# Turning gathered rows on VectorE through DRAM, and moving contexts, key shifts and column sums in a fused cross-attention and mixture-of-experts kernel

## The chip, the cores and the metric

The kernel runs on one core of a Trainium2 chip. The metric is the time of one execution on the device in microseconds (us); the median of several runs counts. The core has five engines that each work through a queue of their own, in order: TensorE (PE), VectorE (DVE), ScalarE (ACT), GpSimd (POOL) and SyncE (SP, which here only issues DMAs). They wait for one another through semaphores. In the profile "PEld" is the loading of weights into TensorE, which overlaps its products.

## The reference

```python
# attention, residual
x = x + x_m          # query = ctx @ Wq.T + bq ; key = ctx @ Wk.T + bk
                     # attention = softmax(query @ key.T) ; x_m = layernorm(x) @ attention.T
# feed-forward on h = layernorm(x): 8 experts, 2 of them for each token
scores = sigmoid(h @ gate_w.T)
_, sel = top_k(scores + expert_bias, 2)
routed_in = h[tok_idx] * scores_sorted[:, None]
routed_out = grouped_swiglu(routed_in, w1, w2, w3, num_tokens_per_expert)   # bf16
shared = silu(h @ sw1.T) * (h @ sw3.T) @ sw2.T                              # f32
x = x + shared.at[tok_idx].add(routed_out)
```

x is 4 batches of 1024 rows of 1024 (f32), the context 4 x 1024 x 512, the head 128 wide, the hidden width 704.

## The kernel before

The kernel has three stages, one after the other on TensorE.

The attention stage (0 to about 650 us) works on tiles of 128 rows, numbered g = 0 to 31, eight to a batch b. It loops over 16 pairs of tiles (p, with g = 2p, and i the place of g in its batch). `product` multiplies a pair by the batch's turned attention matrix `aT` in seven products of halves (`seven`, a scheme that saves the eighth product by adding and subtracting halves): the first and second use the halves themselves and the sums `one`, the third `two`, the fifth the difference that overwrites `b12`, the seventh `four`. After product k the function `then(k)` adds the result to x (line 453), and `between(k)` runs everything else: a step for the tile pair before (its statistics spread over partitions: `masked` on VectorE, `spread` on TensorE, line 485; its turning, `normed` on ScalarE and `turn` on VectorE, line 503; its gate), routing of the pair before that (`route`, some twenty small VectorE instructions, and `weights_of`), loads for the next pair, and the next batch's attention: `looked` (energies on TensorE, line 346, and their maximum on VectorE), `softened` (the exponential on ScalarE), `scaled`, `turned`.

In the last pair of a batch (`last`) the queries and keys of the batch after the next are made: `queries` returns a generator, `half_queries`, whose steps are the products of one half of the context (`pq`, line 329), then its shift by the bias into `qT` and `kT` on VectorE (lines 334 and 336). The contexts come by `load_context` (tiles `ct`, 256 KB each, two buffers for each half of the width). The energies of the next pair need `kT` and the PSUM banks of `pq`.

The column sums of a batch come from `first_sums` (t0), `second_sum` (t1), and `last_sums` (b12 in place, then `four`), on VectorE. PE, DVE, ACT, POOL and SP follow the order of the program here; nothing reorders it.

The shared stage (to about 1459 us) computes the shared expert in f32, in eight slots s of 512 rows: `up(s)` with five rounds f of seven products of 256 columns, and two `down_pair`s. At the same time the rows for the routed experts are collected, by the generator `turns`, one step at each of k = 0, 2 and 4 of a round and at k = 3 of a down pair, from s = 2 on. A step gathers 128 listed rows (bf16, 1024 wide, with the token's number behind) from `xrows` into `xgt` through POOL, turns an earlier block by a DMA transpose from SP (line 1145) into a half `xh` of 256 rows, stores a filled half to `xturned` in DRAM (line 1137), and takes the tokens' numbers out on VectorE (line 1140). There are 92 blocks: 23 slots of four. In a round, VectorE adds `one += pb` (line 1082) after the fourth product and `five += pa` (line 1085) after the fifth; the seventh product writes to `pa` again. `hidden_sums` is eight VectorE additions after the fourth round and again after `up`.

POOL also rewrites the experts' weights in DRAM as bf16 (`pieces`, `convert`, line 255): five experts during the attention stage, three in the first two slots of the shared stage.

The routed stage (to the end) works through the 23 slots of one expert each: it loads the turned rows `xTb`, gathers the expert's weights (line 890), computes in bf16, and adds to the output by indirect DMAs.

Of the kernel before, what the change touches and what calls it, by code (L numbers as in the profile page):

```python
# [83 lines left out]
def xattn_moe_kernel(ctx: ExitStack, tc: tile.TileContext, x, ctxT, wqT, wkT, bqk, gwT, ebias,  # L84
# [30 lines left out]
    tokens_of = [cp.tile([P, NQ], I32, name=f"toks_{i}") for i in range(NS)]  # L115
    xturned = [dram.tile([P, KC, SLOT], BF16, name=f"xturned_{i}") for i in range(NS)]
# [117 lines left out]
    with ExitStack() as a:  # L234
# [14 lines left out]
        def pieces(experts):  # L249

            for e in experts:
                rows = slice(e * P, (e + 1) * P)
                for c in range(KC):
                    cols = slice(c * W13, (c + 1) * W13)
                    nc.gpsimd.dma_start(w13b[rows, cols], w13[rows, cols], max_dma_last_dim=8192)
                    yield
# [122 lines left out]
        def first_sums(b):  # L379
            b11, b12, b21, b22 = quarters(b)  # L380
            one, two = (p4.tile([P, HALF, 512], F32, tag=f"t{i}", name=f"t{i}_{b}")
                        for i in range(2))
            nc.vector.tensor_tensor(one, b12, b11, ALU.subtract)
            t_sums[b] = one, two

        def second_sum(b):
            one, two = t_sums[b][:2]
            nc.vector.tensor_tensor(two, quarters(b)[3], one, ALU.subtract)

        def last_sums(b):  # L390

            b11, b12, b21, b22 = quarters(b)
            four = p3.tile([P, HALF, 512], F32, tag="t4", name=f"t4_{b}", bufs=1)
            two = t_sums[b][1]
            t_sums[b] += four,
            yield
            nc.vector.tensor_tensor(b12, b22, b12, ALU.subtract)
            yield
            nc.vector.tensor_tensor(four, b21, two, ALU.subtract)
# [238 lines left out]
        load(0)  # L638
        with tc.manual_schedule(engines=vector_scalar | {mybir.EngineType.SP}):
# [26 lines left out]
            load(1)  # L666
            norms[1] = statistics(xin[1], "1_1")
            for m in range(LT + 2):
# [8 lines left out]
                if m == LT + 1:  # L677
                    halves = queries(1)
                    next(halves)
                    next(halves)  # L680
                    to_turn(1)
# [6 lines left out]
            for _ in halves:  # L688
                pass
# [3 lines left out]
            first_sums(0)  # L693
            second_sum(0)
# [4 lines left out]
            for p in range(NT // 2):  # L699
# [26 lines left out]
                looked(i)  # L726
                softened(i)
                if i == 0:
                    later = last_sums(b)
                    next(later)  # L730

                def between(k):
                    if 0 < k < NQ + 2:
                        next(converting, None)
                    if k == 0:
                        first_norm(g + 1)
                        if p:
                            masked(g - 2)
                        if i == 0 and b > 0:
                            second_sum(b)  # L740
                        if p > 1:
                            routing[g - 4] = route(g - 4, lgs.pop(g - 4))
                            rows[g - 4] = weights_of(g - 4, routing[g - 4][1])
                        if g + 2 < NT:
# [3 lines left out]
                        if last:  # L748
                            ask_contexts(b + 2, (0, 1))
                    elif k == 1:  # L750
                        if p:
                            spread(g - 2)
                        if ahead:
                            scaled(b + 1, i, on_scalar=True)
                        if p > 1:
                            for v in range(G):
                                weighted(g - 4 + v, *rows[g - 4][v])
                    elif k == 2:
# [9 lines left out]
                        if g + 2 < NT:  # L768
                            load(g + 3)
# [5 lines left out]
                        if i == 0:  # L775
                            next(later)
# [14 lines left out]
                    elif k == 4:  # L791
# [8 lines left out]
                        if i == 0:  # L800
                            next(later, None)
                        if g >= NT - LT:
                            weights_block(2 * (p % 4) + 1)
                    elif k == 5:
# [4 lines left out]
                        if g + 2 < NT:  # L809
                            first_norm(g + 2)  # L810
                            tokens(g + 3)
                            units[0] = row_sums(g + 2)
                    elif k == 6:
# [4 lines left out]
                        if ahead and i + 2 == LT:  # L818
                            first_sums(b + 1)
                        if last:  # L820
                            for _ in halves.pop():
                                pass
                        back(g)
                        back(g + 1)
                        if g + 2 < NT:
                            norms[g + 3] = statistics(xin[g + 3], f"1_{g + 3}")
# [223 lines left out]
    with shared, tc.manual_schedule(engines=vector_scalar | {mybir.EngineType.SP}):  # L1050
# [68 lines left out]
        def turns():  # L1119

            blocks = list(itertools.product(range(NS), range(NQ)))
            asked = []

            def ask(s, q):
                xg = tr.tile([P, ROW], BF16, tag="xg", name=f"xgt_{s}_{q}", bufs=4)
                gather(xg.bitcast(I32), xrows, li[:, s, q : q + 1])
                asked.append(xg)

            for b in blocks[:2]:
                ask(*b)  # L1130
            yield
            done = None
            for j, (s, q) in enumerate(blocks):
                if j + 2 < len(blocks):
                    ask(*blocks[j + 2])
                if done:
                    nc.sync.dma_start(*done)
                    done = None
                xg = asked.pop(0)
                nc.vector.tensor_tensor(tokens_of[s][:, q : q + 1], xg[:, D : D + 2].bitcast(I32),  # L1140
                                        beyond[:, s, q : q + 1], ALU.bitwise_or)
                h, v = divmod(q, 2)
                if v == 0:
                    xh = tr.tile([P, KC, 2 * P], BF16, tag="xh", name=f"xh_{s}_{h}", bufs=2)
                nc.sync.dma_start_transpose(xh[:, :, v * P : (v + 1) * P], xg[:, :D])
                if v:
                    done = xturned[s][:, :, h * 2 * P : (h + 1) * 2 * P], xh
                yield
            nc.sync.dma_start(*done)
# [273 lines left out]
```

## Time and profile before

| | us |
|---|---|
| three runs | 1964.61, 1970.92, 1970.95 |
| median | 1970.92 |
| profiled execution | 1965.19 |
| its span, first to last instruction | 1963.4 |
| TensorE busy | 1894.1 (96%) |
| VectorE, ScalarE, GpSimd busy | 849.5, 511.9, 690.8 |

The page splits the span into 40 slices; "busy" of TensorE is modelled and includes weights that keep it fed. Rows of instructions name the line of the kernel, the engine, the operation, what is written from what is read, and the number of instructions merged into the row. In brackets stand the idle time of the engine just before and what ended it. A DMA row tells what was issued; its landing is listed apart:

```profile
xturned<-xh SPq DMA_DIRECT2D x46, 512.0 KB, 4.1
xq<-in_x_dram SPq DMA_DIRECT2D x128, 128.0 KB, 6.3
ct<-in_ctxT_dram SPq DMA_DIRECT2D x32, 256.0 KB, 4.7
xh<-xgt SPq DMA_TRANSPOSE x92, 6.4
```

The columns are the transfer, the queue, the count, the size of each and the median us from issue to landing.

### The profile page before, as it was taken

The numbers are of one execution on the slowest core, as the hardware profiler recorded it, in microseconds if no ns is written. First come the engines' busy times: TensorE is split into PE (matmuls) and PEld (weight loads), VectorE is DVE, ScalarE is ACT, GpSimd is POOL, SyncE is SP. The second block draws the span as 40 slices with busy tenths as digits, with TensorE's granted clock in tenths as the row PEclk, the third lists the DMA queues.
The fourth block names the chain that finished last, engine by engine and source line by source line (L and its number), as shares of the span: only waits on it lengthen the run. The fifth ranks groups of instructions, "written<-read, shape, count | busy, mean of one in ns | idle before, by whom it ended". The sixth has DMA issues, their size and how long they took to land.

```text
span 1963.4 us, 22795 instructions
## 1 busy us (share of the span) xinstructions
PE 1894.1 (96%) x8000; PEld 1107.4 (56%) x8115; DVE 849.5 (43%) x1977; ACT 511.9 (26%) x884; POOL 690.8 (35%) x753
## 2 busy tenths in 40 slices
PE   7999898899899999999999999999999999999987
PEld 5545444544444448576766667585845565456554
DVE  5665676577876335413231323232233333223332
ACT  3144346165444201010101111010102333223232
POOL 1344364255643151313131312223004444334453
PEclk9999999999999999999999999999999999999999
DMA  8498589589899339497777778686455698559994
GB/s 197 107 237 235 137 252 249 165 219 248 240 267 306 110 101 205 128 223 217 199 185 187 190 198 212 167 189 195 130 222 126 152 271 292 110 161 344 349 327 79
DMA packets 269936, 399.02 MB, mean 203 GB/s; under 512 B 120192, under 2 KB 208768, under 8 KB 259072
## 3 DMA queue, kind: packets, MB, share of 16 engines
q1 hardware_dynamic: 220272, 224.78, 39.6%
q0 software_dynamic: 49552, 172.79, 34.2%
q8 instruction: 65, 1.06, 0.2%
q14 instruction: 47, 0.39, 0.1%
HBM read 322.75 MB, written 174.59 MB: 253 GB/s over the span
## 4 chain that ended last, share of the span: by engine, by line
PE 86%; DMA 5%; DVE 4%; ACT 2%; issue 1%; SPq 1%; POOL 0%; POOLq 0%; DVEq 0%; ACTq 0%
PE pa L135 20%; PE bank L135 15%; PE pc L135 10%; PE bank L1292 7%; PE qa L135 6%; PE pb L135 5%; PE pu L135 4%; PE pq L329 3%; PE qc L135 3%; PE pt_c L135 3%; PE pe L346 2%; DMA x2d<-x 2%; PE qb L135 1%; DMA xq<-in_x_dram 1%; PE pt_a L277 1%
## 5 line engine op out<-in xcount | busy, mean ns | idle before, releaser
L135 PE MATMUL bank<-xTb,w 128*128 128x0 bf16 x2024 | 312.1, 315 | 4.8 <-DMA w<-w13b,wi 2.6
L135 PEld LDWEIGHTS <-w 128*128 128x128 bf16 x2024 | 190.1, 98 | 114.8 <-DMA w<-w13b,wi 2.7
L890 POOL DMA_INDIRECT xgt<-xrows,li x92 | 87.9, 956 | 388.8 <-DMA xh<-xgt 178.1
L1328 POOL DMA_INDIRECT out_dram<-yt,toks x92 | 147.1, 1599 | 144.8 <-DVE yt L1324 89.6
L1292 PE MATMUL bank<-w,hTb 128*128 128x0 bf16 x920 | 163.2, 324 | 0.0
L152 DVE TENSOR_TENSOR hTb<-sg_b,bank 128x512 bf16<-128x512 f32 x115 | 78.8, 687 | 163.3 <-PE bank L135 162.4
L135 PE MATMUL pa<-xs,sw_sb 128*128 128x256 f32 x560 | 132.3, 379 | 0.0
L135 PE MATMUL pa<-aT,xT 128*128 128x512 f32 x256 | 116.4, 597 | 5.5 <-POOL rn L291 3.5
L1292 PEld LDWEIGHTS <-hTb 128*128 128x128 bf16 x920 | 72.1, 97 | 85.8 <-issue 9.9
L135 PEld LDWEIGHTS pa<-xs,sw_sb 128*128 128x128 f32 x560 | 106.4, 190 | 14.5
L1324 DVE COPY yt<-bank 128x512 f32<-128x512 f32 x92 | 61.3, 689 | 120.7 <-PE bank L1292 120.7
L151 ACT ACTIVATE sg_b<-bank 128x512 f32<-128x512 f32 x115 | 68.5, 598 | 165.4 <-PE bank L135 161.3
L291 POOL TENSOR_SCALAR rn<-mv 128x1 f32<-128x1 f32 x64 | 26.4, 413 | 232.0 <-DVE mv L289 226.3
L611 POOL DMA_INDIRECT xrows<-rr,toi x64 | 70.6, 1104 | 96.4 <-DVE toi L584 69.1
L890 POOL DMA_INDIRECT w<-w13b,wi x23 | 22.8, 989 | 204.9 <-PE bank L135 150.8
L287 DVE BATCH_NORM_STATS2 st<-x 128x6 f32<-128x512 f32 x128 | 81.4, 678 | 21.3 <-DMA x<-in_x_dram 20.8
L1326 ACT COPY yt<-bank 128x512 f32<-128x512 f32 x92 | 53.2, 587 | 143.0 <-PE bank L1292 137.0
L453 DVE SCALAR_TENSOR_TENSOR x<-pa,rn,x 128x512 f32<-128x512 f32 x64 | 47.9, 748 | 86.7 <-PE pa L135 84.4
L1173 DVE TENSOR_TENSOR x2c<-x2c,qa 128x512 f32<-128x512 f32 x64 | 43.8, 685 | 92.8 <-PE qa L135 92.8
L172 ACT ACTIVATE st_c<-pt_c 64x256 f32<-64x256 f32 x7 | 2.6, 378 | 311.9 <-PE pt_c L135 311.9
L135 PEld LDWEIGHTS pa<-aT,xT 128*128 128x128 f32 x256 | 48.0, 192 | 61.8 <-issue 54.2
L1082 DVE TENSOR_TENSOR one<-one,pb 128x256 f32<-128x256 f32 x35 | 14.7, 421 | 152.7 <-PE pb L135 152.7
(263 smaller groups left out, 3361.7 us busy)
## 6 DMA issues: line engine op xcount, KB each, us to landing
xturned<-xh SPq DMA_DIRECT2D x46, 512.0 KB, 4.1
xTb<-xturned SPq DMA_DIRECT2D x23, 1024.0 KB, 7.2
w13b<-in_w_dram POOLq DMA_DIRECT2D x64, 352.0 KB, 8.2
x<-in_x_dram SPq DMA_DIRECT2D x32, 512.0 KB, 5.9
xq<-in_x_dram SPq DMA_DIRECT2D x128, 128.0 KB, 6.3
x2d<-x SPq DMA_DIRECT2D x32, 512.0 KB, 6.1
y<-x2d SPq DMA_DIRECT2D x128, 128.0 KB, 3.7
xtd<-xtT SPq DMA_DIRECT2D x16, 1024.0 KB, 4.8
```

What stands on the lines that cost most here:

```text
L135: nc.tensor.matmul(part(pp), w(c), part(xT(c)), start=start and c == 0, stop=c == blocks - 1, skip_group_check=not start)
L151: nc.scalar.activation(sg, pa, AF.Silu)
L152: nc.vector.tensor_tensor(hT[:, f, :], sg, pb, ALU.mult)
L287: nc.vector.bn_stats(st[:, h, :], src[:, h * 512 : (h + 1) * 512])
L329: nc.tensor.matmul(pq[:, i, j, :], w[c // CH][:, c % CH, :], ct[c // CH][:, c % CH, :], start=c == 0, stop=c == CC - 1)
L453: nc.vector.scalar_tensor_tensor(x1[:, cols], py, rs, x1[:, cols], ALU.mult, ALU.add)
L611: nc.gpsimd.indirect_dma_start(out=places[2 * (g + i) + k], out_offset=bass.IndirectOffsetOnAxis(ap=tois[k][:, i : i + 1], axis=0), in_=rr ...
L890: nc.gpsimd.indirect_dma_start(out=dst, out_offset=None, in_=src, in_offset=bass.IndirectOffsetOnAxis(ap=idx, axis=0), **bound)
L1292: nc.tensor.matmul(part(py), hT[:, f, toks], part(w[:, f, cols]), start=False, stop=f == NF - 1, skip_group_check=q < 2)
L1324: nc.vector.tensor_copy(yt[:, q, h * 512 : (h + 1) * 512], py)
L1326: nc.scalar.copy(yt[:, q, h * 512 : (h + 1) * 512], py)
L1328: adds.append([nc.gpsimd.indirect_dma_start(out=outs[q], out_offset=bass.IndirectOffsetOnAxis(ap=toks[:, q : q + 1], axis=0), in_=yt[:, q, ...
```

## The change

Attention stage. The contexts of the next but one batch are asked for one pair earlier (in `between(2)` of the pair with i + 4 = LT, where LT is 8, instead of `between(0)` of the last pair). The last shift of queries and keys runs in `between(5)` of the last pair instead of `between(6)`. The first and second sum are made together, in two halves of 256 columns: one after the third product of the batch's last pair, one after the sixth (after the seventh for the last batch). The third sum (`four`) runs after the second product of a batch's first pair, the fourth (`b12`) where it ran. `masked` stands behind `route` and `weights_of`; the statistics of tile g + 3 stand behind the turning of tile g + 2 in `between(4)` instead of `between(6)`; the load of tile g + 3 stands in `between(1)` instead of `between(2)`. In the first pair the first energies stand behind the first product. Before the loop, tile 1 is loaded right after tile 0, and the queries of batch 1 start one round earlier.

Shared stage. A block is now gathered (three buffers), written to DRAM (`listed`, two steps later), read back in four quarters of 32 partitions (`quarters_of`, two steps later), and turned on VectorE (`turn_block`, two steps later) into `xh`, of which there is one buffer instead of two. VectorE turns within blocks of 32 x 32, so the features of a turned block stand in another order; the rows of `w13b` are written in that same order by `pieces`.

```diff
+    listed = [dram.tile([P, D], BF16, name=f"listed_{i}") for i in range(NS * NQ)]
...
-                    nc.gpsimd.dma_start(w13b[rows, cols], w13[rows, cols], max_dma_last_dim=8192)
+                    h, c = divmod(c, HALF)
+                    src = w13[e * P + c * SQ : e * P + (c + 1) * SQ]
+                    nc.gpsimd.dma_start(
+                        w13b[rows, cols].rearrange("(j f) n -> j f n", j=4),
+                        src.rearrange("f (j h n) -> j h f n", j=4, h=2)[:, h], max_dma_last_dim=8192)
...
-        def first_sums(b):
+        def first_sums(b, part):
+            if b not in t_sums:
+                t_sums[b] = [p4.tile([P, HALF, 512], F32, tag=f"t{i}", name=f"t{i}_{b}")
+                             for i in range(2)]
+            cols = slice(part * 256, (part + 1) * 256)
+            b11, b12, _, b22 = (q[:, :, cols] for q in quarters(b))
+            one, two = (t[:, :, cols] for t in t_sums[b])
             nc.vector.tensor_tensor(one, b12, b11, ALU.subtract)
+            nc.vector.tensor_tensor(two, b22, one, ALU.subtract)
+        def third_sum(b):
+            _, two, four = t_sums[b]
+            nc.vector.tensor_tensor(four, quarters(b)[2], two, ALU.subtract)
+        def fourth_sum(b):
+            b12, b22 = quarters(b)[1::2]
             nc.vector.tensor_tensor(b12, b22, b12, ALU.subtract)
...
         load(0)
+        load(1)
...
-            load(1)
             norms[1] = statistics(xin[1], "1_1")
...
                     if k == 0:
                         first_norm(g + 1)
-                        if p:
-                            masked(g - 2)
-                        if i == 0 and b > 0:
-                            second_sum(b)
                         if p > 1:
                             routing[g - 4] = route(g - 4, lgs.pop(g - 4))
                             rows[g - 4] = weights_of(g - 4, routing[g - 4][1])
+                        if p:
+                            masked(g - 2)
...
-                        if last:
-                            ask_contexts(b + 2, (0, 1))
                     elif k == 1:
...
+                        if i == 0:
+                            third_sum(b)
...
                     elif k == 2:
...
+                            if i + 4 == LT and b + 2 < B:
+                                ask_contexts(b + 2, (0, 1))
...
+                            fourth_sum(b)
+                        if ahead and i + 2 == LT:
+                            first_sums(b + 1, 0)
...
                     elif k == 5:
...
+                        if last:
+                            first_sums(b + 1, 1)
+                            for _ in halves.pop():
+                                pass
                     elif k == 6:
...
-                        if ahead and i + 2 == LT:
-                            first_sums(b + 1)
-                        if last:
-                            for _ in halves.pop():
-                                pass
+                        if ahead and i + 2 == LT and not last:
+                            first_sums(b + 1, 1)
...
-                nc.sync.dma_start_transpose(xh[:, :, v * P : (v + 1) * P], xg[:, :D])
...
+            def ask(n):
+                s, q = blocks[n]
+                gathered[n] = xg = tr.tile([P, ROW], BF16, tag="xg", name=f"xgt_{n}", bufs=3)
+                gather(xg.bitcast(I32), xrows, li[:, s, q : q + 1])
+            def listed_out(n):
+                s, q = blocks[n]
+                xg = gathered.pop(n)
+                nc.sync.dma_start(listed[n], xg[:, :D])
                 nc.vector.tensor_tensor(tokens_of[s][:, q : q + 1], xg[:, D : D + 2].bitcast(I32),
                                         beyond[:, s, q : q + 1], ALU.bitwise_or)
+            def quarters_in(n):
+                quartered[n] = xq = tr.tile([P, 4, D // 4], BF16, tag="xq", name=f"xqt_{n}", bufs=3)
+                quarters_of(xq, listed[n])
+            def turn_block(n):
...
+                    half[s, h] = tr.tile([P, KC, 2 * P], BF16, tag="xh", name=f"xh_{n}", bufs=1)
+                xh = half[s, h]
+                nc.vector.transpose(
+                    xh[:, :, v * P : (v + 1) * P].rearrange("p c (i a) -> p i c a", a=SQ),
+                    quartered.pop(n).rearrange("p i (c f) -> p i c f", f=SQ))
                 if v:
+                    nc.sync.dma_start(xturned[s][:, :, h * 2 * P : (h + 1) * 2 * P],
+                                      half.pop((s, h)))
+            steps = turn_block, quarters_in, listed_out, ask
+            for t in range(len(blocks) + 6):
+                for step, behind in zip(steps, (6, 4, 2, 0)):
+                    if 0 <= t - behind < len(blocks):
+                        step(t - behind)
                 yield
```

## The prediction

> **What bounds the kernel now.** I read the slices first: TensorE (PE) is 96% busy, so time can only come out of its idle stretches or be lost by making new ones. The table of windows says where those lie (columns: stretch, length, then busy us of PE, weight loads, VectorE = DVE, ScalarE = ACT, GpSimd = POOL, granted clock, DMA share, GB/s).
>
> ```profile
> 150.00:200.00 50.00, 46.85 (x169) 25.77 (x168) 29.41 (x75) 20.67 (x34) 21.21 (x32) 0.93 0.85 241
> 200.00:250.00 50.00, 41.41 (x137) 21.87 (x136) 32.68 (x68) 18.50 (x27) 21.04 (x27) 0.93 0.56 151
> ...
> 1000.00:1050.00 50.00, 50.00 (x138) 23.78 (x137) 15.83 (x32) 1.21 (x3) 14.18 (x9) 1.00 0.65 168
> ```
>
> From 0 to 650 us, the attention stage, PE has holes and twice a clock of 0.93. From 650 to 1850 it has almost none: the shared stage has nothing to give and only something to lose. Then the list of PE's own waits (us in total, times, longest):
>
> ```profile
> PE pe L346 <- DVE kT L336: 14.5, 4, 5.7
> PE pq L329 <- DMA ct<-in_ctxT_dram: 12.9, 3, 5.7
> PE pt_a L277 <- DVE at L366: 4.9, 2, 3.1
> PE pa L135 <- DVE t L399: 4.5, 3, 1.5
> ```
>
> These four are what the edits of the attention stage touch. PE's order of time in the pair that ends batch 0 and the next pair's first products (start, duration, idle before in brackets):
>
> ```profile
> 167.53 0.29 PE L485 MATMUL sp<-m,fold 128*128 128x16 f32 x2
> ...
> 180.67 3.75 PE L329 MATMUL pq<-ct,wq_sb 128*128 128x256 f32 x8 [3.15 <-DMA ct<-in_ctxT_dram]
> 184.21 3.11 PE L329 MATMUL pq<-ct,wk_sb 128*128 128x256 f32 x8
> ...
> 188.89 1.89 PE L329 MATMUL pq<-ct,wk_sb 128*128 128x256 f32 x8
> ...
> 216.10 3.75 PE L346 MATMUL pe<-kT,qT 128*128 128x512 f32 x4 [5.70 <-DVE kT L336]
> 219.65 4.18 PE L135 MATMUL pa<-aT,xT 128*128 128x512 f32 x8
> ```
>
> A hole of 3 us or more costs twice: the same products take 3.75 and 3.11 us instead of 1.89 (the clock is 0.50 from 180 to 184 us). After holes of 1.5 us they run at full speed. The Trainium skill says the same with a limit of its own (TensorE: Matmul & The Clock Gate, Part 1: half rate after an idle window of about 3.4 us); these rows set in at 3.15 us, and by the page that loss of 3.1 us would not be certain.
>
> **Attention stage, gains.** (1) Contexts a pair ahead: the holes 3.15 and 5.67 us (the second at 340.13) go, and their slow products: 3.75 + 3.11 - 2 x 1.89 = 3.1, and 3.72 - 1.89 = 1.8. Together 13.7. The four loads (256 KB, 4.7 us from issue to landing) are issued some 30 us earlier; on SP's queue they now stand ahead of a store of xtd, which only the shared stage reads: 4 x 0.5 us late, free. (2) Keys' shifts ahead of the last sum: two holes of 5.70 us behind kT, with 3.75 - 1.88, 4.18 - 3.60 and, at 374.35, 3.68 - 1.88 of slow products: 15.7. In the changed order DVE does the transposes of tokens (1.3), two half sums (2 x 1.15) and then the shifts, while PE runs the second pq (4 x 1.73 = 6.9) and the last product (3.5). DVE has about 6 us of work up to the shifts and 1.5 in them, PE over 10: hidden, with some 2 us to spare. (3) Sums moved up: third sum before group 2 instead of after group 4 removes the three L399 waits (4.5), first and second sum ahead of the next batch remove 0.73 (510.13) and 1.09 (515.01): 6.3. The fourth sum keeps its place, and its waits of 0.55, 0.55 and 1.67 (shown behind rn) stay. (4) First stage: load(1) ahead ends DVE's wait of 3.64 us for x, behind which the first maxima and the 3.07 us hole at 30.86 stand; the first pq fills the hole of 1.78 at 47.83, and pe placed after the first product the 1.59 at 65.18: 6.4. Sum of gains 42.1. (5) Free: the statistics of tile g+3 move from behind the last group to behind group 5, with three steps of POOL (1.06 us) now ahead of the row sums, which end at 207.9 for a product that starts about 8 us later; their load keeps its place on SP, since it waits for the same rows on ACT, and lands some 2 us before DVE comes to it. Without that cover, up to 1.5 us of DVE in a pair.
>
> **Attention stage, loss.** One move is not in the list of words: masked(g-2) now stands behind route and weights_of. Its two small multiplications feed sp, which PE runs right after the second group. DVE in the same pair:
>
> ```profile
> 164.37 0.75 DVE L453 SCALAR_TENSOR_TENSOR x<-pa,rn,x 128x512 f32<-128x512 f32 x1 [0.73 <-PE pa L135]
> 165.04 0.23 DVE L479 TENSOR_TENSOR m<-quarter,rn 128x8 f32<-128x8 f32 x2
> 165.19 0.17 DVE L533 TENSOR_SCALAR ex<-ex 128x16 f32<-128x16 f32 x1
> ...
> 168.95 0.24 DVE L593 TENSOR_TENSOR w<-rn,ss 128x4 f32<-128x4 f32 x2
> ...
> 178.86 1.25 DVE L503 STREAM_TRANSPOSE xtT<-y 128x1024 f32<-128x1024 f32 x1 [1.36 <-ACT y L494]
> ```
>
> Without the masks in front, routing starts at 165.04 and ends at 169.04; the masks end at 169.27. PE reaches sp at 167.53: it waits 1.74 us, with group 3 behind it. The chain starts with PE's own group 1, so an earlier start does not help. Pairs 2 to 15 route, so 14 x 1.74 = 24.4. Lower bound 0 (were PE late by that much for another reason), upper 14 x 2.0. A hole of 1.7 us kept the clock at 249.21 (1.52), so no slow products.
>
> **Shared stage.** Removed: 92 DMA transposes (6.1 us median landing), which only POOL and SP waited for (178 and 125 us); PE is full, so nothing is gained. Added on DVE: 92 transposes of 128x1024. The bf16 one is not in the trace; the f32 one of that shape takes 1.25 us, bounds 0.6 (half the bytes) and 2.5; I take 1.25, 115 us in all, where DVE is busy 16 of 50. Added on SP: 92 stores and 368 quarter loads at about 0.46 us each, 210 us more of its time over 550. New waits on DVE's queue: a transpose waits for four quarters asked two steps before, and the first of each half for the store of the half before it, since xh has one buffer. Behind it on DVE stands `five += pa`, and behind that PE's last group of the same f.
>
> ```profile
> 995.70 0.43 DVE L182 TENSOR_TENSOR hs<-hTc 128x256 f32<-128x256 f32 x1
> ...
> 998.88 0.22 DVE L1140 TENSOR_TENSOR toks<-xgt,beyond 128x1 int32<-128x1 int32 x2
> ...
> 1003.94 0.42 DVE L1085 TENSOR_TENSOR five<-five,pa 128x256 f32<-128x256 f32 x1 [1.30 <-PE pa L135]
> ```
>
> ```profile
> DMA to landing us min/median/max: 3.5/4.9/12.3
> ```
>
> (The second is of the stores into xturned.) The two `toks` show that two steps run back to back at the start of an f. Where these are the second block of a half and the first of the next, in an f without hidden sums: transpose from 959.3 to 960.6, store lands at 965.5, next transpose to 966.8, `one` and `five` to 967.7; PE's last group there starts at 969.14: 1.4 us to spare. In the last f, 3.4 us of hidden sums come first: 998.9 + 1.25 + 4.9 + 1.25 + 0.84 = 1007.1 against 1005.40: about 1.9 us lost. 17 steps in an s is odd, so this falls on s = 2, 4 and 6: 5.7. At the first f of s = 4 and 6, where DVE starts late behind the tails, 0.5 each. Sum 6.7; bounds 0 (store in 3.5) and 43 (rival 3). The end of the pipeline, 97 steps, falls in the fourth f of s = 7, before the slots' weights are asked for: free.
>
> **The conversions of w13.** Each of the 64 keeps its 128 rows and bytes, but its source is now 4 x 32 rows. They land in 4.4 to 18.6 us (median 8.9), nothing of PE waits for one within 600 us, and POOL has 27 us to spare after the 28 of s = 0: 0, upper bound 3. The Trainium skill speaks against it (DMA: Bandwidth & Descriptors, How many engines (k)): a transfer is spread over the largest number up to 16 that divides the slowest dimension of both sides, here 4 instead of 16. By that rule, if a third of the shortest landing of 4.4 us is transfer (an estimate), four times that is some 4 us more of landing; the sum would be the same unless POOL's eight open transfers fill.
>
> **Sum.** 1965.19 - 42.1 + 24.4 + 6.7 = 1954.2, against the profiled execution (span 1963.4, 1.8 around it). The four executions shown (1964.61, 1965.19, 1970.92, 1970.95) average 1967.9, 2.7 above it; I forecast **1957**, 0.7% under the median 1970.92. Its own range: 1948 to 1966.
>
> **Rivals.** (1) The mask costs nothing, because DVE's chain is earlier than I think: 1957 - 24 = 1933. For it: after the move no mask waits on POOL (0.3 to 1.0 us in seven of these pairs). Against: the rows above, in every pair. 0.10. (2) The holes move: contexts, keys and x arrive in time, but DMA, at a share mostly of 0.85 to 1.0 in this stage, or DVE, at 60 to 85%, gives new ones, and half the gain comes back: 1957 + 14 to 21, about 1975, no change. For it: nine DVE waits for x already. Against: no PE wait names a load but ct. 0.22. (3) The other side: the single xh buffer decides. If a store lands 8.5 us after issue, not 4.9, the three last f cost 5.5 each, two first f 4.1 each and eight other f 3.6 - 1.4 = 2.2: 42 instead of 6.7, 1993. Equal to before at about 6.9 us of landing, slower by 0.5% from 7.6. For it: a maximum of 12.3, and 5.5 SP transfers a block instead of 1.5. Against: the removed transposes' packets under 512 B (13,329 for 13 transposes between 855 and 915 us) leave the engines. 0.15. (4) An edit does not reach PE, as contexts held up by SP anyway: 1957 + 14 = 1971. 0.03.
>
> **How the numbers follow.** Forecast 0.50. About 0.5% (10 us) is what a measurement here can tell from no change. Faster by more (under 1961): four fifths of the forecast, rival 1 and some of rival 2: 0.56. Within: 0.28. Slower: rival 3 and the tail of 2: 0.16. Range 1938 to 1980: it leaves out most of rivals 1 and 3.
>
> **What would show it.** PE's waits: no pq <- ct beyond the first, pe <- kT only at 22 us, no t sums; a new `sp` or `pa` wait behind `m` of 1.6 to 1.9 us, 14 times. In the shared stage PE under 50 of 50 in the windows of s = 2, 4, 6 by 2 to 3 us, behind `five`. The landing of stores into xturned and DVE's idle time before the new transposes decide rival 3. The forecast is wrong if sp waits less than 1 us, or if PE loses over 15 us between 830 and 1420.

## The result and the profile after

The changed kernel is slower: 2035.32 us (median of four runs, 2032.56 to 2039.1) against 1967.76 for the kernel before on the same chip, a ratio of 1.035 (95% interval 1.0312 to 1.0389). The prediction was 1957 (1938 to 1980): wrong in sign and far outside its range. Split by the first instruction of each stage on TensorE:

| us in the profiled execution | before | predicted change | after |
|---|---|---|---|
| attention stage (to the first `pu`) | 618.96 | -17.7 | 626.33 (+7.4) |
| shared stage (to the first `bank`) | 840.2 | +6.7 | 901.9 (+61.7) |
| routed stage | 504.2 | 0 | 502.5 |
| span | 1963.4 | | 2030.7 |

So about 25 us are missing in the first stage and 55 in the second. PE's own waits in the changed kernel (us in total, times, longest; line numbers are those of the changed kernel, one to some twenty above those of before):

```profile
PE sp L487 <- DVE m L481: 25.3, 14, 3.5
PE pa L136 <- DVE five L1092: 21.0, 8, 4.1
PE pt_a L282 <- ACT aT L286: 11.6, 3, 6.5
PE pa L136 <- ACT one L1083: 10.0, 3, 4.5
PE qc L136 <- DVE hs L183: 6.7, 2, 3.8
PE pa L136 <- POOL rn L296: 5.2, 4, 3.0
PE pq L334 <- DMA ct<-in_ctxT_dram: 4.3, 1, 4.3
```

Much of the prediction is here: `ct` is awaited once (at the start), `kT` and the column sums `t` have left the list but for the first rounds, and `sp` waits 14 times for the masks, 25.3 us where 24.4 was predicted. Not predicted are `aT` (attention) and `five`, `one` and `hs` (shared). The pair that ends batch 0, which had holes of 3.15 and 5.70 us before, in PE's order of time:

```profile
176.52 0.37 PE L487 MATMUL sp<-m,fold 128*128 128x16 f32 x2 [1.66 <-DVE m L481]
...
186.41 1.89 PE L334 MATMUL pq<-ct,wq_sb 128*128 128x256 f32 x8
188.14 1.89 PE L334 MATMUL pq<-ct,wk_sb 128*128 128x256 f32 x8
...
212.97 1.96 PE L351 MATMUL pe<-kT,qT 128*128 128x512 f32 x4
```

No hole before `pq` or `pe`, and the products run at full speed (1.89 instead of 3.75). The new wait is the predicted one; on VectorE the masks come as the last of the routing:

```profile
175.99 0.23 DVE L595 TENSOR_TENSOR w<-rn,ss 128x4 f32<-128x4 f32 x2
176.14 0.24 DVE L481 TENSOR_TENSOR m<-quarter,rn 128x8 f32<-128x8 f32 x2
```

The windows (stretch, length, busy us of PE, weight loads, DVE, ACT, POOL, then granted clock, DMA share, GB/s):

```profile
150.00:200.00 50.00, 48.34 (x173) 26.18 (x172) 33.27 (x85) 26.05 (x41) 24.22 (x35) 1.00 0.88 237
200.00:250.00 50.00, 45.50 (x169) 23.97 (x168) 38.95 (x82) 19.32 (x29) 24.91 (x37) 1.00 0.75 201
...
1000.00:1050.00 50.00, 45.44 (x159) 29.64 (x157) 25.87 (x51) 4.31 (x11) 17.94 (x13) 0.93 0.72 219
```

Between 150 and 250 us PE won 5.6 us and the clock is back at 1.00. The loss stands in the last line: the shared stage, full before, has holes and a clock of 0.93. Slot by slot it took 103.5 us before for s = 2 to 6 (105.5 for s = 7); after, s = 2 to 7 took 107.2, 117.4, 117.8, 114.5, 117.3 and 110.3.

**Where the new hole of the attention stage comes from.** Around 121 us, all engines of the changed kernel in order of time:

```profile
104.90 0.43 SPq L408 DMA_DIRECT2D x<-in_x_dram  x1
...
117.47 1.28 DVE L292 BATCH_NORM_STATS2 st<-x 128x6 f32<-128x512 f32 x2 [9.03 <-DMA x<-in_x_dram]
...
119.53 0.15 DVE L367 RECIPROCAL rc<-su 128x1 f32<-128x1 f32 x1
...
119.72 1.15 ACT L369 ACTIVATE at<-at,rc 128x1024 f32<-128x1024 f32 x1 [8.07 <-DVE rc L367]
...
120.78 1.05 ACT L286 COPY aT<-pt_a 128x512 f32<-128x512 f32 x2
...
121.39 1.97 PE L282 MATMUL pt_a<-con,at 128*128 128x128 f32 x8 [6.47 <-ACT aT L286]
```

Read it from below: PE waits for ScalarE's copy of `aT`, which stands behind a scaling, which waits for a reciprocal, which stands on VectorE behind statistics, which wait 9 us for a load of x that took over 12 us. Before, `x` was a load of 5.9 us (median). A candidate for what slows it stands in the table of queues, POOL's own (packets, MB, share), before and after:

```profile
q0 software_dynamic: 49552, 172.79, 34.2%
```

```profile
q0 software_dynamic: 74128, 172.89, 33.7%
```

24,576 packets more for 0.10 MB more: 384 for each of the 64 conversions of w13, 512 instead of 128. By the trace's packets the added ones have 4 bytes each.

**Where the holes of the shared stage come from.** Slot s = 4, all engines in order of time:

```profile
1090.62 1.03 SPq L1124 DMA_DIRECT2D x2c<-x2d  x2
...
1091.99 2.13 SPq L419 DMA_DIRECT2D xqt<-listed  x4
...
1095.36 0.53 SPq L1158 DMA_DIRECT2D xturned<-xh  x1
...
1097.93 5.51 SPq L419 DMA_DIRECT2D xqt<-listed  x4
...
1105.25 1.25 DVE L1154 STREAM_TRANSPOSE xh<-xqt 128x1024 bf16<-128x1024 bf16 x1 [8.45 <-DMA xqt<-listed]
...
1106.45 0.41 DVE L1094 TENSOR_TENSOR two<-two,pc 128x256 f32<-128x256 f32 x1
...
1107.22 0.35 ACT L1083 COPY one<-pa 128x256 f32<-128x256 f32 x1
...
1107.63 2.93 PE L136 MATMUL pa<-xs,ws 128*128 128x256 f32 x6 [4.46 <-ACT one L1083]
```

The transpose waits 8.45 us; behind it on VectorE stand the additions that PE's next products need. The name in the brackets is inferred from a semaphore, and each semaphore here serves many transfers in turn (eight for all 987 DMAs of SP), so it can be the wrong one. A DMA raises its semaphore 16 times; counting these updates for each transfer gives the time of its own landing. The quarters of this block are those asked for at 1091.99, and they had landed at 1103.20. The store out of the single `xh`, asked for at 1095.36, landed at 1105.07, 9.7 us later and just ahead of the transpose. So the store ended this wait. The quarters of 1097.93 are the next block's; SP took 5.51 us for them because it waited for the landing of `x2c` first, as it does nine times:

```profile
SPq L419 <- DMA x2c<-x2d: 18.9, 9, 4.3
```

VectorE's waits ahead of its transposes in the changed kernel, under the profile's names:

```profile
DVE xh L1154 <- DMA xturned<-xh: 59.8, 20, 5.5
DVE xh L1154 <- DMA xqt<-listed: 53.5, 25, 9.8
...
DVE xh L1154 <- issue: 39.1, 7, 9.7
```

By the names the store and the quarters look alike in size. By the landings they don't: 133 us in 34 waits ended within 0.3 us of the landing of the store (all 39.1 us of "issue" and half of the 53.5 belong to it), and 27 us in 18 with the quarters, all but the first of these ahead of the second block of a half. Each of the eleven holes of PE above 1 us that are new (1.19 to 4.46 us, 36 us together) ends 2.0 to 3.6 us after the start of a transpose that the store held up. Five of these stores, one in each slot from s = 3 on, landed only 8.6 to 9.7 us after their issue, soon behind the 2 MB of `x2c`; the median store took 4.5.

PE idles 38 us more than before in this stage (holes of 0.3 us or more: 40.9 against 3.0). The other 24 of the 61.7 are products at a lower clock behind the holes (the granted clock is 0.50 in nine stretches of 3.4 or 6.8 us, 47.8 us in all), such as these:

```profile
983.36 3.78 PE L136 MATMUL pa<-xs,sw_sb 128*128 128x256 f32 x8 [2.81 <-DVE five L1092]
986.93 3.17 PE L136 MATMUL pa<-xb,sw_sb 128*128 128x256 f32 x8
989.94 1.89 PE L136 MATMUL pc<-xs,ws 128*128 128x256 f32 x8
```

### The profile page after: what moved, and what is told of

Its sections match the earlier page's. It is cut to its first block, busy times and chain, and to the rows that moved or that the text cites. A ratio compares the mean times of both kernels' runs of the same rounds, so it can differ in the third digit from the quotient of the medians.

```text
span 2030.7 us, 23574 instructions
## 1 busy us (share of the span) xinstructions
PE 1918.6 (94%) x8000; PEld 1117.8 (55%) x8115; DVE 956.7 (47%) x2077; ACT 512.4 (25%) x884; POOL 698.4 (34%) x753
## 5 line engine op out<-in xcount | busy, mean ns | idle before, releaser
L1154 DVE STREAM_TRANSPOSE xh<-xqt 128x1024 bf16<-128x1024 bf16 x92 | 114.1, 1242 | 160.6 <-DMA xturned<-xh 59.8
L136 PE MATMUL pa<-xs,sw_sb 128*128 128x256 f32 x560 | 141.6, 399 | 21.1 <-DVE five L1092 21.0
L136 PEld LDWEIGHTS pa<-xs,sw_sb 128*128 128x128 f32 x560 | 111.0, 200 | 40.5 <-DVE five L1092 24.7
L296 POOL TENSOR_SCALAR rn<-mv 128x1 f32<-128x1 f32 x64 | 25.1, 392 | 250.2 <-DVE mv L294 243.9
L613 POOL DMA_INDIRECT xrows<-rr,toi x64 | 66.1, 1033 | 89.5 <-DVE toi L586 54.3
L455 DVE SCALAR_TENSOR_TENSOR x<-pa,rn,x 128x512 f32<-128x512 f32 x64 | 47.8, 747 | 97.1 <-PE pa L136 97.0
L607 ACT ACTIVATE rr<-x,w 128x1024 bf16<-128x1024 f32 x64 | 74.0, 1226 | 33.2 <-DVE w L595 33.2
```

The costliest lines, as they stand in the source:

```text
L136: nc.tensor.matmul(part(pp), w(c), part(xT(c)), start=start and c == 0, stop=c == blocks - 1, skip_group_check=not start)
L607: nc.scalar.activation(rr[:, k, :D], x2, AF.Identity, bias=w[:, 1, k : k + 1], scale=w[:, 0, k : k + 1])
L613: nc.gpsimd.indirect_dma_start(out=places[2 * (g + i) + k], out_offset=bass.IndirectOffsetOnAxis(ap=tois[k][:, i : i + 1], axis=0), in_=rr ...
L1154: nc.vector.transpose(xh[:, :, v * P : (v + 1) * P].rearrange("p c (i a) -> p i c a", a=SQ), quartered.pop(n).rearrange("p i (c f) -> p i ...
```

## The experiments

All stages in us, from one profiled execution of each kernel; the ratio is to the kernel before on the same chip, with its 95% interval.

| kernel | attention | shared | median | ratio |
|---|---|---|---|---|
| before | 618.96 | 840.2 | 1967.76 | |
| after | 626.33 | 901.9 | 2035.32 | 1.035 (1.0312 to 1.0389) |
| mask_front | 620.63 | 901.2 | 2025.49 | 1.0289 (1.0263 to 1.0316) |
| dma_turns | 606.25 | 841.9 | 1956.42 | 0.9947 (0.993 to 0.9964) |
| dma_turns_split | 623.45 | 844.3 | 1976.22 | 1.0047 (1.003 to 1.0064) |
| dve_turns_only | 657.32 | 904.6 | 2069.63 | 1.0531 (1.0502 to 1.0561) |
| best | 592.36 | 840.2 | 1939.5 | 0.9857 (0.9831 to 0.9884) |
| mask_w32 | 592.49 | 907.6 | 2004.77 | 1.0168 (1.0135 to 1.0202) |
| w32_blocks | 593.57 | 883.5 | 1977.84 | 1.005 (1.0032 to 1.0069) |
| w32_order | 593.24 | 902.4 | 2005.75 | 1.0187 (1.0155 to 1.0219) |
| blocks_order | 593.37 | 856.1 | 1957.35 | 0.9959 (0.9944 to 0.9974) |
| blocks_order_x2act | 592.04 | 861.7 | 1956.37 | 0.9945 (0.9924 to 0.9967) |
| blocks_order_qact | 597.75 | 864.7 | 1964.25 | 0.9985 (0.997 to 1.0) |
| best_stats | 581.22 | 847.9 | 1935.32 | 0.9835 (0.9816 to 0.9855) |
| dma_turns_stats | 606.35 | 840.2 | 1953.78 | 0.9945 (0.9926 to 0.9964) |

The six kernels from mask_w32 to blocks_order_qact have the same attention stage; it took 592.04 to 597.75. The shared stage of kernels with DMA transposes is 840.2 in three, 841.9, 844.3 and 847.9 in others. A difference of 5 us in one profile is therefore no evidence.

**The masks, alone.** The changed kernel with `masked` in front of routing:

```diff
                         first_norm(g + 1)
+                        if p:
+                            masked(g - 2)
                         if p > 1:
                             routing[g - 4] = route(g - 4, lgs.pop(g - 4))
                             rows[g - 4] = weights_of(g - 4, routing[g - 4][1])
-                        if p:
-                            masked(g - 2)
```

> The changed kernel with one edit undone: the masks again in front of routing. Theory (the masks' place costs PE its wait at sp, 25.3 us in 14 pairs of the changed kernel's profile): sp waits fall to almost nothing, the attention stage ends some 25 us earlier (626 to about 601), the shared stage is unchanged at about 902; time about 2034 - 25 = 2009. Rival (VectorE does the same work in each pair, so PE only waits later, at another result of VectorE): less than 10 us gained, 2024 to 2034, with new waits of PE behind x or aT.

The waits behind `m` went (0.6 us left), but the stage only won 5.7 us: waits behind `aT` rose from 11.6 to 19.1 us and those behind `rn` from 5.2 to 9.5. The rival holds here: with x late, the masks' wait had covered others.

**The attention edits without the shared stage's, and the conversions.** dma_turns takes `turns`, `listed` and the w13 conversion from the kernel before; dma_turns_split takes only `turns` and `listed` from it; dve_turns_only is the kernel before with these three parts of the change.

```diff
-                    h, c = divmod(c, HALF)
-                    src = w13[e * P + c * SQ : e * P + (c + 1) * SQ]
-                    nc.gpsimd.dma_start(
-                        w13b[rows, cols].rearrange("(j f) n -> j f n", j=4),
-                        src.rearrange("f (j h n) -> j h f n", j=4, h=2)[:, h], max_dma_last_dim=8192)
+                    nc.gpsimd.dma_start(w13b[rows, cols], w13[rows, cols], max_dma_last_dim=8192)
...
-                nc.vector.transpose(
-                    xh[:, :, v * P : (v + 1) * P].rearrange("p c (i a) -> p i c a", a=SQ),
-                    quartered.pop(n).rearrange("p i (c f) -> p i c f", f=SQ))
+                nc.sync.dma_start_transpose(xh[:, :, v * P : (v + 1) * P], xg[:, :D])
```

> All edits of the attention stage, but blocks turned by DMA transposes and w13 converted with 128 rows as source, as before the change. Theory (the late x loads in the changed kernel's attention stage come from the conversions with 4 x 32 rows): the attention stage ends at 600 to 610 instead of 626, the shared stage takes 840, time 1950 to 1960. Rival (the late loads come from the attention edits themselves, from the order of loads on SP): the stage ends at about 626 as in the changed kernel, time about 1968 + 7 = 1975.

> As dma_turns, but w13 converted with 4 x 32 rows as source, as in the changed kernel (DMA transposes keep the old order of features, so the routed experts' products use w13 rows in another order than the turned rows; the output differs, the work doesn't). Theory: the attention stage ends at about 626, some 20 us later than in dma_turns, with a wait of PE of 6 us near 121 behind aT, VectorE waiting up to 9 us for x; time about 1975. Rival (conversions cost 0 to 3, as predicted): the same as dma_turns within 3 us.

> The kernel before with the shared stage's edits alone (blocks turned on VectorE through DRAM, w13 converted with 4 x 32 rows). Theory: the shared stage takes about 902 instead of 840 (+62), and the attention stage is 5 to 20 us longer through the conversions: 1968 + 67 to 82 = 2035 to 2050. Rival (the shared stage is slow only in company of the attention edits, or the conversions cost nothing): attention 619 as before, 2030 or less.

The theory holds in the first two. In dve_turns_only it holds for the shared stage (904.6 for about 902), but the attention stage lost 38.4 us where 5 to 20 were expected, and the time lies above the range. With the old conversions the stage ends at 606.25, 20.1 us before the changed kernel's; putting the new conversions back alone costs 17.2 us of stage and 20 us of time, with PE waiting 4.5 us behind `aT` at 120.07. VectorE's waits for x in dma_turns and dma_turns_split:

```profile
DVE st L287 <- DMA x<-in_x_dram: 7.5, 4, 3.1
```

```profile
DVE st L291 <- DMA x<-in_x_dram: 36.6, 9, 7.1
```

So what the conversions cost depends on what PE waits for anyway: 17 to 20 us here, 28.3 with the masks in front (mask_front against best, below). In the order of the kernel before they cost 38.4 us (657.32): PE there waits 26.6 us for `ct` instead of 12.9, and 19.7 behind `aT`. The shared stage takes its 60 us or more with either attention stage (901.9, 904.6).

**Another form of the same conversions, and the masks with x in time.** best is dma_turns with `masked` in front. mask_w32 is mask_front with

```diff
-                        w13b[rows, cols].rearrange("(j f) n -> j f n", j=4),
-                        src.rearrange("f (j h n) -> j h f n", j=4, h=2)[:, h], max_dma_last_dim=8192)
+                        w13b[rows, cols].rearrange("(j f) n -> f j n", j=4),
+                        src.rearrange("f (j h n) -> h f j n", j=4, h=2)[h], max_dma_last_dim=8192)
```

> All edits of the attention stage but the masks' place, which is again in front of routing; blocks turned by DMA transposes and w13 converted with 128 rows as source. Theory (the masks cost PE 24.2 us of waits at sp in dma_turns, and nothing else takes their place): the attention stage ends at 606 - 24 = 582, time about 1956 - 24 = 1932. Rival (as with mask_front, where 25 us of waits at sp went and only 6 us of the stage with them, because PE then waits for other results of VectorE): the stage ends at about 600, time 1948.

> mask_front (the changed kernel with the masks in front) with the same conversions of w13 written with the 32 features as the outer dimension and the 4 blocks inside. Theory (what slows the loads of x is that a conversion with 4 as its outer dimension is spread over few DMA engines): the attention stage ends as in best, at 582 to 600 instead of 620.6; the shared stage stays at 901; time 1990 to 2005. Rival (it is the number of packets of a conversion, 512 instead of 128, which stays): 620, time 2025.

mask_w32 writes the same rows to the same places and ends the stage at 592.49, as best does (592.36). The line of POOL's queue in mask_w32 tells why the experiment can't separate its two theories:

```profile
q0 software_dynamic: 49552, 172.79, 33.7%
```

The packets fell back to those of before. The cost is thus shown to lie in the form with 4 as the outer dimension, and not in the new order of rows. The traces speak for few engines rather than for packets, although no run separates the two. The added packets carry 4 bytes each. And of the 16 updates of a conversion's semaphore (medians, from issue) the first and last came after 6.8 and 8.1 us before the change and 6.4 and 7.8 in mask_w32, but after 3.9 and 13.3 in the changed kernel: part of the transfer's pieces finish early and part very late. By the Trainium skill (DMA: Bandwidth & Descriptors, How many engines (k)) such a transfer runs on 4 engines instead of 16; the spread agrees with it, but no row here counts engines.

best won 13.9 us of stage over dma_turns, between its two expectations. So something else took 10 of the 24.

**The statistics.** best_stats is best, and dma_turns_stats is dma_turns, with one line moved back behind the last group:

```diff
                             tokens(g + 2)
-                            norms[g + 3] = statistics(xin[g + 3], f"1_{g + 3}")
...
                         back(g)
                         back(g + 1)
+                        if g + 2 < NT:
+                            norms[g + 3] = statistics(xin[g + 3], f"1_{g + 3}")
```

> best (attention edits without the masks' move, DMA transposes) with the statistics of tile g+3 again behind the last group of a pair instead of behind the fifth. Theory (the move is free, as predicted): the attention stage stays at 592 within 2 us. Rival (the statistics in the middle of a pair make VectorE wait for x, and give back part of the 24 us that the masks' place should bring and of which only 14 came): 580 to 588.

> dma_turns (all attention edits, masks behind routing, DMA transposes) with the statistics of tile g+3 again behind the last group; with dma_turns, best and best_stats it completes the square of masks and statistics. Theory (the masks cost 24 alone, and while PE waits for them the statistics are hidden: the two losses overlap, 14 + 11 = 25 with masks taken out first): the attention stage ends at 603 to 607, as in dma_turns (606.25). Rival (the two losses are independent, 14 and 11): 595.

In the four profiles the stage ends at 606.25 (masks and statistics as in the change), 606.35 (statistics back), 592.36 (masks back), 581.22 (both back). The statistics' place costs nothing while PE waits for the masks, and 11 us when it doesn't; the masks cost 25 once the statistics are back. The medians give less for the last step, 4 us with intervals that overlap (0.9857 and 0.9835); the late gathers of rows in slot s = 2 of best_stats's profile (+5.8) are part of that. best_stats beats both kernels: 1935.32 us, 1.65% under the kernel before.

**The shared stage: the buffer and the order on SP.** w32_blocks gives each block its own store and two buffers of one block:

```diff
-                if v == 0:
-                    half[s, h] = tr.tile([P, KC, 2 * P], BF16, tag="xh", name=f"xh_{n}", bufs=1)
-                xh = half[s, h]
+                xh = tr.tile([P, KC, P], BF16, tag="xh", name=f"xh_{n}", bufs=2)
...
-                if v:
-                    nc.sync.dma_start(xturned[s][:, :, h * 2 * P : (h + 1) * 2 * P],
-                                      half.pop((s, h)))
+                nc.sync.dma_start(xturned[s][:, :, q * P : (q + 1) * P], xh)
```

w32_order turns the order within a step round; blocks_order has both edits:

```diff
-            steps = turn_block, quarters_in, listed_out, ask
+            steps = quarters_in, listed_out, ask, turn_block
...
-                for step, behind in zip(steps, (6, 4, 2, 0)):
+                for step, behind in zip(steps, (4, 2, 0, 6)):
```

> mask_w32 with the turned rows in two buffers of one block each, every block stored by itself (the same room in SBUF as one buffer of two blocks; 46 more stores of half the size). Theory A (the single buffer: VectorE's 59.8 us in 20 waits for the store into xturned are what holds PE): the shared stage falls from 901 to 870 or less. Theory B (the quarters come late, because SP is behind: 53.5 us in 25 waits): more stores make it worse or leave it, 895 to 910.

> mask_w32 with the order within a step turned round: quarters, list, gather first, then the transpose and its store, so that SP no longer waits for VectorE's transpose before it asks for quarters. Theory B (quarters late, since SP stands at the store of the turned rows until VectorE has turned them): the shared stage falls from 901 to 870 or less. Theory A (single buffer): unchanged within 10 us, since the store still lands after the next transpose of VectorE would start.

> w32_blocks and w32_order together: blocks of their own, and quarters, list and gather ahead of the transpose and its store. Theory (in w32_blocks SP stands at the store of a block until VectorE has turned it, so quarters are asked late after the hidden sums, as at 982.27 us for a transpose at 988.72): the shared stage falls from 883.5 to 865 to 872. Rival (the loads of quarters themselves take too long, from the loads of x2c and from a full queue): 880 or more.

Against mask_w32 (907.6) the buffers alone win 24 us, less than theory A asked for; the order alone wins 5, as theory A said (unchanged within 10) and no more than two profiles of one stage differ by (901.2 and 907.6); the two together win 51.5, more than expected. The medians say the same with other sizes: 27, nothing, and about 41 by the ratios. VectorE's waits ahead of the transposes say why. In w32_blocks no store holds it, and the quarters hold it longer than ever. In w32_order the names are mixed, but by the landings all 152 us in 37 waits ended with the store. In blocks_order both are small (by the landings 31 us are the store's). In this order:

```profile
DVE xh L1151 <- DMA xqt<-listed: 94.8, 39, 7.8
```

```profile
DVE xh L1154 <- DMA xqt<-listed: 90.4, 23, 7.7
DVE xh L1154 <- DMA xturned<-xh: 34.0, 8, 9.3
DVE xh L1154 <- issue: 27.5, 6, 9.0
```

```profile
DVE xh L1151 <- DMA xqt<-listed: 22.2, 9, 4.7
...
DVE xh L1151 <- DMA xturned<-xh: 10.5, 11, 1.6
```

The two form a ring: SP stands at the store until VectorE has turned the block, and only then asks for the quarters of a later block, for which VectorE waits in its turn. Either link is enough to hold VectorE, so taking out one leaves the other. A delay from anywhere (the hidden sums, 2 MB of `x2c`) goes round. An example from w32_blocks, where the hidden sums hold VectorE to 980.43:

```profile
977.86 0.38 SPq L1140 DMA_DIRECT2D listed<-xgt  x1
981.70 0.53 SPq L1154 DMA_DIRECT2D xturned<-xh  x1
982.27 2.20 SPq L419 DMA_DIRECT2D xqt<-listed  x4
```

SP is idle for 3.5 us, asks at 982.27, and VectorE's next transpose starts at 988.72, 5.14 us late. The median landing stayed short, with exceptions behind `x2c` as above. In mask_w32 (transfer, queue, count, size of each, median us from issue to landing):

```profile
xqt<-listed SPq DMA_DIRECT2D x368, 64.0 KB, 4.2
xturned<-xh SPq DMA_DIRECT2D x46, 512.0 KB, 4.2
```

**Another queue.** blocks_order with two loads or with the quarters issued by ScalarE:

```diff
-                nc.sync.dma_start(x2s[u], x2d[2 * s + u].rearrange("(v p) d -> p v d", v=2))
+                nc.scalar.dma_start(x2s[u], x2d[2 * s + u].rearrange("(v p) d -> p v d", v=2))
```

```diff
-                nc.sync.dma_start(dst[j * SQ : (j + 1) * SQ], src[j])
+                eng.dma_start(dst[j * SQ : (j + 1) * SQ], src[j])
...
-                quarters_of(xq, listed[n])
+                quarters_of(xq, listed[n], nc.scalar)
```

> blocks_order with the loads of the residual rows (x2c, two of 1 MB in the second round of each slot) on ScalarE's queue instead of SP's. Theory (four quarter loads behind the x2c loads took 5.2 us to be issued at 940.08 in w32_blocks, against 2.2 elsewhere, because SP's queue was held by them): the shared stage falls by another 12 to 20, to 850 to 858. Rival (both queues share the engines that move data, so the quarters come as late): within 5 us of blocks_order.

> blocks_order with the quarter loads on ScalarE's queue instead of SP's. Theory (it is SP's queue, about 5 us of issuing in a step of 4.6, that makes the quarters late): the shared stage falls to 845 to 855. Rival (ScalarE waits for the stores into listed, and holds the copies of one, five and two): 880 or more, with waits of PE behind ScalarE.

Neither gain came: 861.7 and 864.7 against 856.1. But neither run shows that SP's queue does not limit, because neither freed SP or VectorE. With the loads on ScalarE's queue SP waits for their landing as long as before, since they still share its eight semaphores; with the quarters there, ScalarE's copies wait for the quarters, as the rival said, though the stage lost less than it asked for. First SP's wait in blocks_order and blocks_order_x2act, then ScalarE's in blocks_order_qact:

```profile
SPq L419 <- DMA x2c<-x2d: 30.2, 12, 4.9
SPq L419 <- DMA x2c<-x2d: 29.7, 6, 6.8
```

```profile
ACT one L1090 <- DMA xqt<-listed: 63.0, 13, 7.5
```

What keeps the stage of blocks_order 16 us above 840 stays open. PE's holes there sum to 11.7 us more than before, the longest new one 1.78; in the five kernels with DMA transposes they sum to at most 4.3 us more.

## Why the prediction was wrong, step by step

**Attention, gains (1) to (4), 42.1: right but for 4.** With masks and statistics in their old places and the old conversions, the stage ends 37.7 us earlier (581.22). Of step (4), the holes of 1.78 and 1.59 us did not go (1.73 at 53.23 and 1.59 at 62.80 in best_stats), and the last batch's wait behind `rn` is 3.69 us where it was 1.67; that is 5.4 us, the missing 4.4 within what one profile tells.

**Step (5), "free": right in the changed kernel, for a reason not given.** The statistics cost nothing there because PE waits for the masks. Without that cover they cost 11 us by the profile (4 by the medians); the text had asked for "up to 1.5 us of DVE in a pair", which is 22.5 in 15 pairs.

**Attention, loss, 24.4: right.** 25.3 us in 14 waits, and 25.1 of stage between best_stats and dma_turns_stats. Rival 1 fell.

**"The conversions of w13 ... 0, upper bound 3": failed.** They cost 20.1 us (626.33 against 606.25; 17 to 38 in other company). The step asked who waits for a conversion, and rightly found nobody; it did not ask whose transfers share the DMA engines with it. Loads of x came up to 9 us late, and through statistics, reciprocal, scaling and copy they reached PE. It had the rule that speaks against the edit before it, turned it into 4 us of landing for the conversion itself (measured: 13.3 instead of 8.1 in the median, by the semaphores), and left the neighbours out. That is also what rival 2 (new holes from late loads) amounts to; it blamed full DMA engines in general and not the conversions, so its 14 to 21 us meet the 20.1 by luck.

**"Shared stage ... Sum 6.7; bounds 0 and 43": failed, measured 61.7.** The single prices were good: a transpose of 128x1024 bf16 took 1.24 us (1.25 assumed), a store of a half landed in 4.5 in the median (4.9). (The 1.9 us for a last f should have been 1.7 by its own sum, which changes little.) Two things were missing. First, the path: the store was to delay PE in five rounds, by 1.9 or 0.5 us each, and "four quarters asked two steps before" were taken as there in time. In the changed kernel the store held VectorE 34 times, and eleven of these are followed by a hole of PE of more than 1 us, 36 us in all; five of the eleven come behind `x2c`, which the sum does not have. SP's 210 us of issues were counted as a sum over 550, but not put in line: the store of the turned rows, which waits for VectorE, stands ahead of the next quarters. So the path was a ring and not a queue, and the rows of mask_w32, w32_blocks and blocks_order show that neither of its two links alone is the cost (24 and 5 of 51.5). Second, a hole here was priced at its length; most holes of 2.8 us and more also slowed the products behind them, 24 of the 61.7 us, though the prediction's own first rows showed that a hole can cost twice. (Not every one does: after 3.07 us at 30.86 of the kernel before, and after 3.19 us at 912.79 of the changed one, the products ran at full speed.)

**Rivals.** Rival 3 had the side and the cause: the single buffer decided. Its condition (a landing of 8.5 us) came true for five of the 45 stores whose landing the trace tells, and its 42 us were too few because the ring, which delays the store's issue, and the slow clock were left out. Rival 4 fell for the contexts: PE waits for `ct` only at the start.

**The sum** would have been, with the two terms as measured, 1965.19 - 42.1 + 24.4 + 20.1 + 61.7 = 2029.3 for a profiled execution that gave 2032.56.

## What to carry to other kernels

When a transfer is reshaped, ask not only who waits for it but whose transfers run beside it, and look at its packets and at how far its completions spread: here the same bytes with 32 instead of 4 as the outer dimension cost nothing. When one engine issues loads and stores of a pipeline in order, draw the ring: a store that waits for an engine must not stand ahead of the loads which that engine waits for. And two waits that lie side by side hide one another, so undoing one edit shows less than it costs; undo them in pairs. And before a wait is blamed on the transfer that the profile names, look when that transfer landed.

## What the runs showed of the hardware

A conversion from f32 to bf16 in DRAM of 128 rows of 1408 made 128 packets, 512 with its outer dimension 4 (the added 384 of 4 bytes each), and again 128 with 32 outside and 4 inside; POOL took 583, 737 and 594 ns to issue one. VectorE's transpose of 128x1024 in bf16 takes 1.24 us, no less than the 1.25 of f32. A hole of 2.81 us on TensorE was enough to slow the next sixteen products of 256 columns (3.78 and 3.17 us for eight instead of 1.89). The length alone does not decide: 2.03 us at 1462.48 of mask_w32 slowed four products of 512 columns (3.49 us), while 2.05 us at 1441.13 of w32_blocks (1.96 us), 3.19 us at 912.79 of the changed kernel and 3.67 us at 1066.30 of w32_blocks (1.99 us each for eight of 256) did not. Four loads of 64 KB took SP 2.0 to 4.2 us to issue between 950 and 1070 us of the changed kernel, and 5.1 and 5.5 us soon behind two loads of 1 MB (at 972.40 and 1097.93); in and ahead of the second, SP waited 5.0 us for these loads to land.
